# The 128 gram products of an image: three groups at every second quarter step in place of six groups at every quarter

## The chip, the cores and the metric

The kernel runs on one core of a Trainium2 chip. The metric is the device time of one execution in microseconds, the median of several executions. One profiled execution gives the page and the trace. Names: PE is TensorE (PEld its weight loads), DVE is VectorE, ACT is ScalarE, POOL is GpSimd, SP is the engine that issues most DMAs.

## The reference, cut to what matters

The input x has 16 images of 64 channels and 128 x 128 pixels, in float32. Four layers follow each other; each adds its result to x, after a group norm of 32 groups:

```python
# layer 0: gram matrix of the normalised image, applied to the image
gram = jnp.einsum('bcn,bdn->bcd', xf, xf) / N
y = jnp.einsum('bcd,bdn->bcn', gram, xf)
out = jnp.einsum('oc,bchw->bohw', conv_w, y)
...
x = x + _L0_conv_ref(_gn(x), L0_conv_conv_w)
x = x + _L1_conv_ref(_gn(x))          # |gx| + |gy| of a Scharr filter per channel
x = x + _L2_conv_ref(_gn(x), L2_conv_W, L2_conv_b)    # shift of half the channels, 3x3 convolution
x = x + _L3_conv_ref(_gn(x), ...)     # 3x3 and 1x1 convolution, batch norm over all images, clip
```

The change concerns the gram matrix alone: per image a 64 x 65 sum over 16384 pixels (the 65th column gives the channel sums).

## The kernel before, in words

An image is cut into NS = 8 chunks of R = 8 rows in each of its two halves. The main loop (lines 911 to 950) walks over steps, and in each step over four quarters, q = 0 to 3. In every quarter it calls, in this order, what each live stage has to do there: Layer3, Layer2, Front (layer 0's application and layer 1, with `sobel`), and last `Gram` (lines 926 to 930); then `tick()` (line 931) moves the small chains of statistics on by one link. Layer3 of image b starts at step 35 + 8b, Layer2 at 25 + 8b, Front at 15 + 8b (line 861), so that in the middle of the run one chunk of each of them is worked on in every step. All engines keep the order of the program (`InOrder`, line 63).

What PE gets in one step of the middle of the run, by quarter:
- q0, Layer3 (lines 814 to 821): `shared` into `one`, 6 matmuls, and `own` into `two[:, 0]`, 5 matmuls: 11.
- q1, Layer3 `own` into `two[:, 1]`, 5 matmuls (line 825), and Front `mix` into `po`, 2 matmuls (line 509): 7. In the last step before an image's grams two small ones for `pe` come along (line 508).
- q2, Layer2 `shared` and `own` (lines 742 to 747): 11.
- q3, Layer2 `own` (line 761), 5, and `mix` (line 524), 2: 7.

Every matmul has 128 rows of weights and 64 columns, and writes one half of the 128 output partitions. `issue` (lines 591 to 601) puts the two halves in turn, beginning with the half that was not used last (`last[0]`), so that two matmuls can run side by side. `own` (lines 611 to 620) has 3 matmuls on one half and 2 on the other.

DVE in the same step: at q0 `sobel`'s first two operations, the addition of edges to `two`, x3, and the difference d2 (line 702); at q1 four operations of `sobel`; at q2 Layer3's y (line 842), which reads `two` of q0 and q1, and d3; at q3 the second d3 and, after everything else, the difference d2 that the next q2 reads (line 769). This last one overwrites the buffer that q2's `own` matmuls read. ACT copies `po` into `xh` (lines 475 to 481), which frees the single `po` buffer for the next `mix`, and `one` into c (lines 767 and 828), which frees the single `one`.

`Gram` of an image (lines 407 to 444) loads eight slabs of x over SP, and ACT copies them into `xw`; at its step 8 and in the first half of its step 9 PE multiplies `xw` with itself, 128 matmuls of 64 columns of weights against 65 columns, accumulated in `pg`. They are put in groups at the end of quarters, after the work of the other stages. `n` counts quarters from step 8; at n = 6 `gram_chain` begins, with a DVE copy of `pg`. The next image's copies into `xw` begin at q3 of that step 9.

`pace` (lines 871 to 877) gives images 1 to 6 two sub-steps per quarter, so that two values of n fall into one quarter; images 0 and 7 to 15 have one. The gram step of images 7 to 15 is step 46, 54, ... 110 of the main loop, with all stages at work.

After the last y (step 163) come the batch norm's sums and a last stage of loads, one ACT and one DVE operation per part, and stores (lines 986 to 994).

Of the kernel before, what the change touches and what calls it, by code (L numbers as in the profile page):

```python
# [108 lines left out]
def tile_kernel(ctx: ExitStack, tc: tile.TileContext, x, cw_h, w2_t, b2, wbin_t, w1_t, b1, gamma, beta, consts, out):  # L109
# [297 lines left out]
    class Gram:  # L407
# [5 lines left out]
        def at(self, i, q):  # L413
            b = self.b
            CG = C // 8
            if i < NS:
                if q == 0 and i != 1:
                    for m in range(i + (1 if i == 2 else 2) if i else 0, min(i + 3, NS)):
                        t = xin.tile([P, CG, W], F32, tag="xr", name=f"xr_{b}_{m}", bufs=3)
                        sp.dma_start(t, x[b].rearrange("c h w -> h c w")[:, m * CG:(m + 1) * CG, :])  # L420
                        self.xr[m] = t

                if q == 3 and i > 0:
                    for m in (0, 1) if i == 1 else (i,):
                        act.copy(
                            xw[:, :, m * CG:(m + 1) * CG, :].rearrange("p w c t -> p c w t"),
                            self.xr.pop(m).rearrange("p c (w t) -> p c w t", t=2),
                        )
                return
            n = 4 * (i - NS) + q  # L430
            if n == 0:
                self.pg = ps_g.tile([P, CP, W], F32, tag="g", name=f"pg_{b}")[:, 0, 0:C + 1]

            for _ in range(22 if n < 4 else 20 if n < 6 else 0):
                w = self.w
                s = w % 2
                pe.matmul(
                    self.pg[s * C:(s + 1) * C, :], xw[:, w // 2, 0:C, s], xw[:, w // 2, :, s],
                    start=(w < 2), stop=(w >= W - 2),
                )  # L440
                last[0] = s
                self.w += 1
            if n == 6:
                chains.append(gram_chain(b, self.pg))
# [180 lines left out]
    class Layer2:  # L625
# [7 lines left out]
        def load(self, i):  # L633


            b = self.b
            N = (R + 1) * W + 2
            t = ring.tile([P, N], F32, tag="v2", name=f"v2_{b}_{i}", bufs=3)
            for c0, c1, shift in ((0, C // 4, 1), (C // 4, C // 2, -1), (C // 2, C, 0)):
                cut = R * W + 1 - shift  # L640
                parts = [(0, i * R, N)] if i + 1 < NS else [(0, i * R, cut), (cut, -R, N)]
                for at, j, end in parts:
                    for s in range(2):

                        first = j * W + at - 1 + shift
                        src = x2_d[b][W + first:W + first + 2 * C * PLANE].rearrange("(c s n) -> s c n", s=2, n=PLANE)
                        sp.dma_start(t[s * C + c0:s * C + c1, at:end], src[s, c0:c1, 0:end - at])
            self.v[i] = t[:, 1:N - 1].rearrange("p (j w) -> p j w", w=W)
            self.whole[i] = t
# [223 lines left out]
    for b in range(B):  # L873
        half = 1 <= b <= 2 * EARLY
        pace[b] = at, 2 if half else 1

        at += (NS // 2 if half else NS) + {0: 4, 2 * EARLY: 2}.get(b, 0)
# [33 lines left out]
    for step in range(steps):  # L911
        for q in range(4):
# [13 lines left out]
            for b in range(B):  # L926
                at, n = pace[b]
                for m in range(n):
                    v = 4 * n * (step - at) + n * q + m
                    run(Gram, b, v // 4, v % 4)  # L930
# [13 lines left out]
            if step >= last_one and q == 2:  # L944

                n = 3 if step == last_one else 1 if step < last_one + NS - 2 else 0
# [86 lines left out]
```

## Time and profile before

| | us |
|---|---|
| median of 3 runs | 2819.88 (2819.15 to 2820.23) |
| the profiled execution | 2818.68 |
| its span in the trace | 2816.9 |
| PE busy, weight loads busy | 2237.6, 1153.6 |
| DVE, ACT, POOL busy | 2201.0, 2121.1, 887.5 |
| first gram burst of images 7, 8, ... 15 begins at | 520.1, 658.7, 797.2, 935.7, 1074.2, 1213.0, 1352.1, 1490.6, 1629.1 |
| last stage, DMAs alone (2345 to 2817) | 472, at 402 GB/s |

Almost every instruction is recorded by one helper (line 73), so groups are told apart by their tiles: `pg<-xw` are the gram products, `two<-d,w`, `two<-qd,pk`, `two<-d,wi` the `own` matmuls, `one<-v,...` the `shared` ones, `po<-x,abd` is `mix`. Every matmul in float32 shows as two records. A record's length is not its share of PE's time, since matmuls are pipelined: the distance between starts is. In a line of the timeline the first number is the start, the second the length from the first start to the last end, then engine, line, operation and tiles, xcount; a bracket gives the idle time before it and what ended it, as inferred from semaphores. In a line of the waits stand the total, the number of times and the longest.

### The profile page before, as it was taken

The numbers are of one execution on the slowest core, as the hardware profiler recorded it, in microseconds if no ns is written. First come the engines' busy times: TensorE is split into PE (matmuls) and PEld (weight loads), VectorE is DVE, ScalarE is ACT, GpSimd is POOL, SyncE is SP. The second block draws the span as 40 slices with busy tenths as digits, with TensorE's granted clock in tenths as the row PEclk, the third lists the DMA queues.
The fourth block names the chain that finished last, engine by engine and source line by source line (L and its number), as shares of the span: only waits on it lengthen the run. The fifth ranks groups of instructions, "written<-read, shape, count | busy, mean of one in ns | idle before, by whom it ended". The sixth has DMA issues, their size and how long they took to land. (4 is left out here: it accounts for less than half of the span.)

```text
span 2816.9 us, 46299 instructions
## 1 busy us (share of the span) xinstructions
PE 2237.6 (79%) x14772; PEld 1153.6 (41%) x14772; DVE 2201.0 (78%) x3758; ACT 2121.1 (75%) x3171; POOL 887.5 (32%) x1326
## 2 busy tenths in 40 slices
PE   4568899999999999999999999999999995000000
PEld 2323444545554545353635363466666542000000
DVE  3999999898989898989898989999997435333332
ACT  4666779888888888888888888998997668333332
POOL 1035433343434343434343434454444310000000
PEclk7679999999999999999999999999999998555555
DMA  6789978888888888888888877787877767999999
GB/s 167 193 221 228 236 192 241 214 229 207 229 208 225 217 220 215 219 218 218 217 219 213 226 182 193 206 212 202 216 207 189 208 195 266 419 420 420 420 420 391
DMA packets 688880, 685.95 MB, mean 244 GB/s; under 512 B 61744, under 2 KB 590144, under 8 KB 688640
## 3 DMA queue, kind: packets, MB, share of 16 engines
q1 hardware_dynamic: 662656, 614.42, 73.6%
q0 software_dynamic: 24576, 68.12, 9.9%
q8 instruction: 119, 1.95, 0.3%
q14 instruction: 121, 0.99, 0.1%
q10 hardware_dynamic: 1408, 0.46, 0.1%
HBM read 346.23 MB, written 268.44 MB: 218 GB/s over the span
## 5 line engine op out<-in xcount | busy, mean ns | idle before, releaser
L73 PE MATMUL two<-d,w 128*64 128x508 f32 (+2 forms) x2560 | 889.8, 586 | 0.0
L73 PE MATMUL two<-d,wi 128*64 128x508 f32 (+3 forms) x1536 | 618.4, 577 | 0.0
L73 POOL DMA_DIRECT2D qd<-d x512 | 270.3, 530 | 867.1 <-issue 324.6
L73 PE MATMUL two<-qd,pk 128*64 128x512 f32 (+1 forms) x1024 | 518.9, 588 | 3.7 <-DMA qd<-d 3.0
L73 POOL TENSOR_SCALAR edges<-v,co 64x8 f32<-64x8 f32 x512 | 353.9, 691 | 357.5 <-ACT v L73 244.8
L73 PEld LDWEIGHTS two<-d,w 128*64 128x64 f32 x2560 | 303.3, 136 | 281.0 <-issue 200.3
L73 PE MATMUL po<-x,abd 128*64 128x512 f32 x1024 | 368.9, 631 | 60.6 <-ACT xh L73 60.6
L73 DVE TENSOR_TENSOR d<-v 128x512 f32<-128x512 f32 (+1 forms) x512 | 346.3, 679 | 75.5 <-issue 36.3
L73 PE MATMUL one<-v,w 128*64 128x508 f32 (+2 forms) x1600 | 391.8, 578 | 0.0
L73 PE MATMUL one<-v,wi 128*64 128x508 f32 (+3 forms) x1536 | 390.1, 593 | 0.0
L73 ACT COPY qd<-d 64x512 f32<-64x512 f32 x512 | 315.2, 616 | 21.0 <-DVE d L73 14.5
L73 DVE SCALAR_TENSOR_TENSOR e<-e 128x1032 f32<-128x1032 f32 (+1 forms) x256 | 313.0, 1223 | 0.0
L73 ACT ACTIVATE xh<-po,co 128x128 f32<-128x128 f32 (+1 forms) x480 | 275.3, 621 | 39.3 <-PE po L73 37.2
L73 PEld LDWEIGHTS two<-d,wi 128*64 128x64 f32 x1536 | 194.6, 135 | 146.2 <-issue 100.2
L73 DVE SCALAR_TENSOR_TENSOR y<-two,c 128x1024 f32<-128x1024 f32 x128 | 155.9, 1218 | 122.8 <-ACT v L73 65.8
L73 POOL TENSOR_SCALAR v<-v,kc 128x9 f32<-128x9 f32 x256 | 247.3, 980 | 12.0
L73 PEld LDWEIGHTS one<-v,w 128*64 128x64 f32 x1600 | 169.4, 137 | 160.4 <-issue 99.5
L73 ACT ACTIVATE v<-x,co 128x512 f32<-128x512 f32 (+2 forms) x368 | 234.8, 704 | 0.0
L73 PEld LDWEIGHTS one<-v,wi 128*64 128x64 f32 x1536 | 162.3, 138 | 154.9 <-issue 113.0
L73 ACT ACTIVATE u<-u 128x1024 f32<-128x1024 f32 x128 | 135.5, 1058 | 97.3 <-DVE u L73 96.8
L73 DVE SCALAR_TENSOR_TENSOR u<-xh 128x1170 f32<-128x1170 f32 x128 | 175.5, 1371 | 12.2 <-ACT xh L73 9.8
L73 PEld LDWEIGHTS pg<-xw 128*64 128x64 f32 x4096 | 161.6, 143 | 46.4 <-issue 38.6
(154 smaller groups left out, 3424.7 us busy)
## 6 DMA issues: line engine op xcount, KB each, us to landing
xr<-in_x SPq DMA_DIRECT2D x128, 512.0 KB, 6.9
x<-in_x SPq DMA_DIRECT2D x256, 256.0 KB, 4.2
x_d<-u SPq DMA_DIRECT2D x512, 128.0 KB, 3.6
y_d<-y SPq DMA_DIRECT2D x512, 128.0 KB, 4.2
x_d<-x SPq DMA_DIRECT2D x496, 128.0 KB, 2.5
qd<-d POOLq DMA_DIRECT2D x256, 130.0 KB, 3.0
qd<-d POOLq DMA_DIRECT2D x256, 129.8 KB, 3.7
v<-x_d SPq DMA_DIRECT2D x448, 72.1 KB, 3.0
```

The lines of the kernel that those rows point to most:

```text
L73: return self.tc.keep_in_program_order(call(*args, **kwargs))
```

## The change

The groups 22, 22, 22, 22, 20, 20 at n = 0 to 5 become 44, 42, 42 at n = 0, 2, 4. In a step and a half of images 7 to 15 the grams of q1 now stand at the end of q0, those of q3 at the end of q2, and those of the next q1 at the end of the next q0. Within each group the order of the products and of the halves is unchanged, and `gram_chain` still begins at n = 6.

```diff
             if n == 0:
                 self.pg = ps_g.tile([P, CP, W], F32, tag="g", name=f"pg_{b}")[:, 0, 0:C + 1]
 
-            for _ in range(22 if n < 4 else 20 if n < 6 else 0):
+            for _ in range({0: 44, 2: 42, 4: 42}.get(n, 0)):
                 w = self.w
                 s = w % 2
                 pe.matmul(
```

## Prediction

> **What bounds the kernel now.** I first read the page's 40 slices (TensorE, PE below, and VectorE, DVE, at 8 to 9 tenths from slice 4 to 32; after 2345 us the DMAs alone), then busy time by stretch, then the waits of one image's period. The gram bursts of images 7 to 15 begin every 138.5 us (520.1, 658.7, 797.2 ... 1629.1 us); I read the one at 797 us. q0 to q3 are a step's quarters; q0' and q1' are those of the next step. The gram step and a half runs from q0 at 792.90 to q2' at 825.94; the step before it has no grams.
>
> ```profile
> core 0: us, PE busy (x) PEld busy (x) DVE busy (x) ACT busy (x) POOL busy (x), PEclk, DMA share, GB/s
> 777.28:792.90 15.62, 15.62 (x79) 5.31 (x77) 15.25 (x22) 15.46 (x26) 7.41 (x10) 1.00 0.81 212
> 792.90:825.94 33.04, 33.04 (x368) 20.22 (x365) 26.20 (x35) 27.86 (x43) 10.58 (x20) 1.00 0.88 225
> ```
>
> The gram step leaves DVE and ACT idle; the step before it fills all three. The waits of DVE, then of PE, from 797 to 936:
>
> ```profile
> DVE y L73 <- ACT e L73: 4.0, 1, 4.0
> DVE d L73 <- issue: 3.5, 2, 1.8
> DVE d L73 <- POOL v L73: 0.8, 2, 0.5
> DVE two L73 <- PE two L73: 0.7, 1, 0.7
> ```
> ```profile
> PE po L73 <- ACT xh L73: 1.4, 1, 1.4
> ```
>
> So one image is a loop of two halves: PE sets the pace through the grams, DVE then works without pause, and PE meets it again in one wait of 1.35 us (at 914.89). Where PE hands over is in DVE's timeline:
>
> ```profile
> 824.19 1.23 DVE L73 SCALAR_TENSOR_TENSOR y<-two,c 128x1024 f32<-128x1024 f32 x1 [4.01 <-ACT e L73]
> ...
> 828.38 1.28 DVE L73 SCALAR_TENSOR_TENSOR u<-e,co,u 128x1024 f32<-128x1024 f32 x1
> 829.58 0.08 DVE L73 DVE_READ_ACCUMULATOR u<-e,co,u 128x1 f32 x1
> 831.36 0.56 DVE L73 TENSOR_TENSOR d<-v 128x384 f32<-128x384 f32 x1 [1.70 <-issue]
> ```
>
> The page names ACT e, done at 823.61; but y reads `two`, whose last q1' matmul starts at 823.50, lasts 0.59 and ends at 824.09, 0.10 before y. The d at 831.36 overwrites what q2' of PE reads, whose last matmul ends at 831.27. From there to 914.89 DVE is busy 81.0 of 83.5 us. So two dates set the period: **y** (end of q1') and **d** (end of q2'), with 1.70 us of slack between y's block and d.
>
> Now the joint between a quarter's work and its grams, PE's timeline at q0:
>
> ```profile
> 796.32 1.44 PE L73 MATMUL two<-d,w 128*64 128x508 f32 x5
> 797.17 0.34 PE L73 MATMUL pg<-xw 128*64 128x65 f32 x2
> 797.60 0.59 PE L73 MATMUL two<-d,w 128*64 128x508 f32 x1
> 798.02 1.55 PE L73 MATMUL pg<-xw 128*64 128x65 f32 x42
> 799.35 0.59 PE L73 MATMUL two<-d,w 128*64 128x512 f32 x1
> ```
>
> Each matmul is two records on one 64-column half of the array; two matmuls on different halves run side by side. Quarter q0 has 11 matmuls, an odd number: the last one (797.17 and 797.60) runs alone, with only one gram matmul (2 records) beside it, and the other grams begin when it is done.
>
> **What the Trainium skill says.** "TensorEngine Tiling (Array Packing)", Key Properties: tiles work independently and run matmuls in parallel. The trace agrees: pairs start within 0.01 us of each other. "TensorE: Matmul & The Clock Gate", Part 3, The mechanism, says that matmuls start and end strictly in program order; here the trace shows a little more freedom (2 to 4 gram records start before an earlier-issued matmul's last record), and the trace decides. The same page's table of specifications gives VectorE and ScalarE a strict first-in first-out queue: so everything on DVE behind y waits with it. The trace agrees (nothing in DVE's 4.01 us).
>
> **Prices.** A big matmul pair takes 0.853 us (795.46 to 796.32), so 0.427 per matmul. A gram matmul costs 0.063: 44 of them between two even pairs run from 282.17 to 284.94, 2.77 us, and the pair after them takes 0.86, as if no grams were there:
>
> ```profile
> 282.17 2.95 PE L73 MATMUL pg<-xw 128*64 128x65 f32 x88
> 284.94 1.03 PE L73 MATMUL po<-x,abd 128*64 128x512 f32 x4
> 285.80 2.94 PE L73 MATMUL pg<-xw 128*64 128x65 f32 x88
> ```
>
> So 22 grams are 1.39, 42 are 2.65, 20 are 1.26. What a quarter takes beyond that is the joint. The starts of q0, q1, q2, q3, q0', q1', q2' are 792.90, 799.35, 803.97, 810.43, 815.04, 821.37, 825.94. q0: 6.45 - 11 x 0.427 - 1.39 = 0.37. q1 (7 matmuls): 4.62 - 2.99 - 1.39 = 0.24. q2 0.38, q3 0.23, q0' 0.37 (20 grams), q1' 0.32, of which about 0.1 is a small statistics product. All six segments are odd; together about 1.9 us per image.
>
> **The change, part by part.**
> *Images 0 to 6.* Image 0's grams stand in one burst with no work between (256 records from 27.0 us). Images 1 to 6 run two sub-steps per quarter, so their groups are already 44, 44, 40 and become 44, 42, 42: 2 matmuls, 0.13 us, at most 0.8 us in six images; I take nothing.
> *The joints (nine images).* With grams after q0, q2 and q0' only, the segments are q1+q2 and q3+q0', 18 matmuls each, even. The joint at q0 stays (its segment begins long before, at the last product that spans both halves). The joints of q1, q2, q3 and q0', 0.24 + 0.38 + 0.23 + 0.37 = 1.22 us, go. Bounds of an even joint that isn't shown in this stage: nothing (the row at 284.94) to 0.2.
> *The grams that move ahead of q1'.* Before, 108 stand ahead of it; now all 128: +20 x 0.063 = 1.26 us. So **q1' starts at 821.37 - 1.22 + 1.26 = 821.41**. Its five Layer3 matmuls end at 824.13, y starts at 824.23: +0.04. In the first gram step the 22 grams moved ahead of q1 make y there 0.9 later and the grams moved ahead of q3 make `two` 0.6 later; both lie before the 4.01 us wait and are lost in it.
> *After y.* DVE's block from y to 829.66 ends at 829.70. PE reaches the end of q2' at 821.41 + 18 x 0.427 + 0.1 + 0.16 = 829.36 instead of 831.27, since q1' no longer has grams behind it. So **d starts at 829.74 instead of 831.36: -1.62 us**, and DVE's block, not PE, is now what ends last. ACT: its c (828.93, wait 0.96 on PE) and u (841.76, wait 0.62 on DVE) can move by 1.58 together, about the same.
> *Queues passed.* The grams issue no DMA. Their readers gain nothing: gs stays in its place (no wait at 827.65), ACT's xw copies at 831.83 wait for nothing. ACT work of q1 and q3 fed by the later matmuls (xh) has waits of 0.34 to 1.67 us ahead of it and lies before y or in its shadow.
> *Behind d.* DVE's 83.5 us up to PE's wait at 914.89 move as a whole. PE is ahead by 1.35 there; in its stretch after q1' it may lose one half slot (0.43) at the next product that spans both halves, which that lead hides. Without the lead it would cost 0.43 per image.
>
> Sum: -1.62 x 9 = **-14.6 us**. The profiled execution took 2818.7 (span 2816.9 and 1.8 around it): 2804.1. The median shown, 2819.9, is 1.2 higher: 2805.3; I say **2805**. The last stage (472 us, DMA share 1.00) is fixed in length and begins after the last y, so it moves along and hides nothing.
>
> **Rivals.**
> *More (B).* The half slot at q0 goes as well, if the halves arrive there in step: 0.37 more at y and d, -2.0 x 9 = -18: 2802; with a shorter DVE block down to 2799. Against: the profile shows the odd matmul at q0, and the work before it isn't changed.
> *Nothing (C).* The joints stay, as halves that are out of step lose the same half slots elsewhere. Then y is 1.26 later, its slack of 1.70 takes that, PE's d is unmoved: 2820. For: q1's five matmuls after grams run 0 1 0 1 1 by halves, out of step. Against: such a stream runs in the trace (po beside one at 858.57) at 0.427.
> *Slower (D).* A gram costs what a group's row suggests, 2.35 / 22 = 0.107, wherever it stands, and nothing is saved. Then y is 20 x 0.107 = 2.14 late, past the 1.58 that ACT and the 1.70 that DVE can take: +0.57 per image, 2825. It decides from y late by 1.6 on. Against: 44 in 2.77 us at 282.
>
> **Numbers.** Forecast (A) 0.64, own range 2801 to 2811 (even joints 0 to 0.2, three of them); B 0.12; C 0.14; D 0.10. A measurement here can tell about 0.2%, 5.6 us. A and B are faster: 0.76; C and half of D same: 0.18; rest slower: 0.06. Range 2799 to 2820: A, most of B, two thirds of C, 0.83.
>
> **What would show it.** Gram groups of 2.65 to 2.8 us without a lone two record beside them after q2 and q0'; q0 to q2' near 31.5 instead of 33.04; DVE's y wait still near 4 less 0.6, the wait of d gone or under 0.2; period near 136.9; PE's wait on xh still there. A y wait over 5 us makes D right; a period of 138.5, C. Wrong too if DVE finds a new wait in its long stretch.

## The result, and the profile after

| | before | after |
|---|---|---|
| median of 6 runs each, us | 2819.99 (2817.85 to 2820.28) | 2804.82 (2800.37 to 2805.94) |
| the profiled execution, us | 2818.68 | 2800.37 |
| its span in the trace, us | 2816.9 | 2798.6 |
| distance from one image's first gram burst to the next, us (images 7 to 15) | 138.51 to 139.05 | 136.76 to 137.33 |

The ratio is 0.9942, 95% interval 0.9931 to 0.9953: faster, by 0.58% in that ratio and by 15.2 us, or 0.54%, in the medians. The prediction was 2805. The profiled execution of the changed kernel is the fastest of its six; the extra 3.3 us lie before image 7, whose first burst begins at 516.8 instead of 520.1 us. Experiment e5 below shows that the change has no part in that, so the analysis goes by distances within one image. These give 13.8 us over the eight distances from image 7 to image 15 and 1.2 us after that.

The same image as before, by stretch: a step without grams, then from q0 to the start of q2', then DVE's long stretch from d to PE's restart:

```profile
core 0: us, PE busy (x) PEld busy (x) DVE busy (x) ACT busy (x) POOL busy (x), PEclk, DMA share, GB/s
770.46:786.08 15.62, 15.62 (x78) 5.21 (x76) 15.25 (x22) 15.46 (x26) 7.40 (x10) 1.00 0.79 209
786.08:817.33 31.25, 31.25 (x368) 17.62 (x365) 24.46 (x32) 26.92 (x41) 8.45 (x20) 1.00 0.86 217
822.86:906.37 83.51, 82.50 (x452) 36.81 (x448) 80.99 (x163) 75.89 (x119) 34.02 (x52) 1.00 0.85 224
```

The step without grams takes 15.62 us as before, and DVE's stretch 83.51 instead of 83.53. All of the gain is in the gram steps: from q0 to the start of q2' they take 31.25 us instead of 33.04.

The waits of DVE and then of PE in one image's period, from the first burst at 790.4 to the next at 927.2:

```profile
DVE y L73 <- ACT junk L73: 3.4, 1, 3.4
DVE two L73 <- PE two L73: 2.0, 1, 2.0
DVE y L73 <- ACT v L73: 0.9, 1, 0.9
DVE d L73 <- POOL v L73: 0.7, 2, 0.5
DVE d L73 <- issue: 0.3, 1, 0.3
```
```profile
PE po L73 <- ACT xh L73: 1.0, 1, 1.0
```

The wait of 4.0 in front of y is 3.4, `two` waits 2.0 instead of 0.7, and of d's two waits (1.8 and 1.7 before) 0.3 is left, the one of the first gram step. The wait for PE in front of the second d is gone, as DVE's timeline shows:

```profile
817.46 1.22 DVE L73 SCALAR_TENSOR_TENSOR y<-two,c 128x1024 f32<-128x1024 f32 x1 [3.44 <-ACT junk L73]
...
821.65 1.28 DVE L73 SCALAR_TENSOR_TENSOR u<-e,co,u 128x1024 f32<-128x1024 f32 x1
822.86 0.08 DVE L73 DVE_READ_ACCUMULATOR u<-e,co,u 128x1 f32 x1
822.86 0.56 DVE L73 TENSOR_TENSOR d<-v 128x384 f32<-128x384 f32 x1
```

No bracket stands on d: DVE goes from u straight to it. Now the joints on PE. Before the change the one of q2 looked like that of q0, a lone record with a single gram matmul beside it:

```profile
808.25 0.59 PE L73 MATMUL two<-d,wi 128*64 128x508 f32 x1
808.45 0.28 PE L73 MATMUL pg<-xw 128*64 128x65 f32 x2
808.68 0.59 PE L73 MATMUL two<-d,wi 128*64 128x508 f32 x1
809.11 1.49 PE L73 MATMUL pg<-xw 128*64 128x65 f32 x41
```

After the change, at q0 and at q2:

```profile
790.36 0.34 PE L73 MATMUL pg<-xw 128*64 128x65 f32 x2
790.78 0.59 PE L73 MATMUL two<-d,w 128*64 128x508 f32 x1
791.21 2.93 PE L73 MATMUL pg<-xw 128*64 128x65 f32 x86
793.94 0.59 PE L73 MATMUL two<-d,w 128*64 128x512 f32 x1
...
801.23 0.59 PE L73 MATMUL two<-d,w 128*64 128x508 f32 x1
801.26 0.59 PE L73 MATMUL two<-d,wi 128*64 128x508 f32 x1
801.65 2.79 PE L73 MATMUL pg<-xw 128*64 128x65 f32 x83
804.27 0.60 PE L73 MATMUL two<-d,wi 128*64 128x512 f32 x1
```

At q0 a lone `two` record still holds 86 of the 88 gram records back (790.78). At q2 the last two big records start side by side (801.23 and 801.26) and the grams follow 0.4 later, when both halves are free: 42 products take 2.62 us from 801.65 to the next big matmul.

### The profile page after: what moved, and what is told of

Its sections match the earlier page's. It is cut to its first block, busy times and chain, and to the rows that moved or that the text cites. A ratio compares the mean times of both kernels' runs of the same rounds, so it can differ in the third digit from the quotient of the medians.

```text
span 2798.6 us, 46299 instructions
## 1 busy us (share of the span) xinstructions
PE 2222.1 (79%) x14772; PEld 1088.8 (39%) x14772; DVE 2201.4 (79%) x3758; ACT 2120.1 (76%) x3171; POOL 859.5 (31%) x1326
## 5 line engine op out<-in xcount | busy, mean ns | idle before, releaser
L73 PE MATMUL two<-d,wi 128*64 128x508 f32 (+3 forms) x1536 | 626.6, 576 | 0.0
L73 POOL TENSOR_SCALAR edges<-v,co 64x8 f32<-64x8 f32 x512 | 335.2, 655 | 352.5 <-ACT v L73 244.4
L73 PE MATMUL po<-x,abd 128*64 128x512 f32 x1024 | 386.2, 631 | 60.4 <-ACT xh L73 60.4
L73 PE MATMUL one<-v,w 128*64 128x508 f32 (+2 forms) x1600 | 409.0, 578 | 0.0
L73 PE MATMUL one<-v,wi 128*64 128x508 f32 (+3 forms) x1536 | 407.4, 590 | 0.0
L73 POOL TENSOR_SCALAR v<-v,kc 128x9 f32<-128x9 f32 x256 | 238.4, 944 | 11.9
L73 PEld LDWEIGHTS one<-v,w 128*64 128x64 f32 x1600 | 163.3, 137 | 177.4 <-issue 130.0
L73 PEld LDWEIGHTS one<-v,wi 128*64 128x64 f32 x1536 | 156.0, 138 | 162.6 <-issue 126.4
L73 ACT ACTIVATE u<-u 128x1024 f32<-128x1024 f32 x128 | 135.4, 1058 | 90.3 <-DVE u L73 89.9
L73 PEld LDWEIGHTS po<-x,abd 128*64 128x64 f32 x1024 | 111.0, 140 | 175.4 <-ACT xh L73 92.3
```

What stands on the lines that cost most here:

```text
L73: return self.tc.keep_in_program_order(call(*args, **kwargs))
```

## The experiments

My theory has two parts. **Joints:** a group of grams costs most of a half slot wherever an odd number of big matmuls stands before it. (A lone big matmul takes as long as a pair, 0.85 us, and leaves the other half of the array empty; a half slot is the 0.43 us lost by that.) **Two dates:** the period follows y (the end of q1' on PE, then DVE's block) or d (the end of q2' on PE), whichever is later. The first rival is that fewer groups are better in themselves; the second, that y's later date is what holds the change back. In the first set (e1 to e4) the kernel before took 2820.09 us, in the second (e5 to e7) 2820.47, in the third (e8 and e9) 2819.54.

The period is the median of the eight distances from one image's first gram burst to the next; for e6 the range is given.

| | groups in images 7 to 15 | us | ratio to before, 95% | period, us |
|---|---|---|---|---|
| change | q0 44, q2 42, q0' 42 | 2804.8 | 0.9931 to 0.9953 | 136.8 |
| e1 | q1 44, q3 42, q1' 42 | 2804.1 | 0.9929 to 0.9957 | 136.7 |
| e2 | q0 44, q1 42, q2 42 | 2810.6 | 0.9955 to 0.9980 | 137.4 |
| e3 | six as before, idle half first | 2803.1 | 0.9928 to 0.9953 | 136.7 |
| e4 | q0 44, q2 42, q0' 22, q1' 20 | 2808.6 | 0.9949 to 0.9974 | 137.3 |
| e5 | six as before | 2820.2 | 0.9989 to 1.0005 | 138.6 |
| e6 | q0 128 | 2824.0 | 1.0008 to 1.0021 | 136.7 to 143.5 |
| e7 | q1 44, q3 42, q2' 42, chain later | 2790.1 | 0.9877 to 0.9908 | 135.4 |
| e8 | q0 64, q0' 64 | 2804.4 | 0.9931 to 0.9958 | 136.7 |
| e9 | as e1, chain later | 2794.9 | 0.9897 to 0.9924 | 136.0 |

### e1: the same three groups one quarter later

```diff
-            for _ in range({0: 44, 2: 42, 4: 42}.get(n, 0)):
+            for _ in range({1: 44, 3: 42, 5: 42}.get(n, 0)):
```

> Three groups, 44, 42, 42, at n = 1, 3, 5, at the ends of q1, q3 and q1'. Joint theory (a group costs a half slot of 0.24 to 0.38 us where an odd number of big matmuls stands between it and the last point at which both halves were in step): every segment now has 18 matmuls, q0's joint goes as well, all 1.8 us per image are saved on PE; y has only 86 grams ahead of it and comes about 3 us earlier against q0, so that d has a wait again, about 2.9 us, and PE's end of q2' sets it: period 138.53 - 1.81 = 136.7, time 2803 to 2804. Rival, that fewer groups save a fixed price each: as the change, 2805, with q0's joint no cheaper. Rival, that y's date is what limits the change: y is freed here, and the time falls below 2800.

Measured: 2804.06, period 136.65 to 137.20. Counted from q0, y comes at 27.89 us instead of 31.29 (about 3 us earlier was expected); DVE waits 2.04 in front of it, and 2.69 in front of d (expected about 2.9). All joints are even (no lone record stands beside the grams), and PE's date for d sets the period again. y is early and it doesn't help: the rival that y's date alone holds the change back, with a time below 2800, falls. The time can't tell the joints from a fixed price per group here (2804.06 and 2804.82); e2 and e3 do.

### e2: three groups again, at odd joints

```diff
-            for _ in range({0: 44, 2: 42, 4: 42}.get(n, 0)):
+            early = {0: 44, 2: 42, 4: 42}
+            late = {0: 44, 1: 42, 2: 42}
+            for _ in range((early if b < 7 else late).get(n, 0)):
```

> Images 7 to 15: also three groups, 44, 42, 42, but at n = 0, 1, 2, at the ends of q0, q1 and q2; images 0 to 6 as in the changed kernel. Joint theory: the joints of q0, q1 and q2 stay odd (0.37 + 0.24 + 0.38), only those of q3, q0' and q1' go; all 128 grams stand ahead of q1', so y is 1.26 - 0.60 = 0.66 later and d 0.8 to 0.95 earlier: 2811 to 2813. Rival, that the number of groups is what counts: 2805, as the change.

Measured: 2810.62, a little below the expected range: y comes 0.68 us later than before (expected 0.66) and d 1.11 us earlier (expected 0.8 to 0.95). With the same number and the same sizes of groups, about 6 us of the change's 15 are gone, as the joints say; the interval (0.9955 to 0.9980) and the change's (0.9931 to 0.9953) lie side by side without meeting, and the periods are 137.4 and 136.8. The number of groups is not what counts.

### e3: six groups at their old places, only the order of the halves changed

Against the kernel before the change:

```diff
-            for _ in range(22 if n < 4 else 20 if n < 6 else 0):
-                w = self.w
-                s = w % 2
+            count = 22 if n < 4 else 20 if n < 6 else 0
+            first = 6 if count and b > 6 else 0
+            halves = [1 - n % 2] * first + [0, 1] * ((count - first) // 2)
+            for s in halves:
+                w = self.done[s]
```

(xw is then indexed with w, start is w == 0 and stop the 64th product of a half; `done` counts per half.)

> The six groups of before at their old places, 22, 22, 22, 22, 20, 20; only within a group of images 7 to 15 the order differs: six products of the half that the odd big matmul leaves idle come first, then pairs. Joint theory: six instead of one or two gram products run in the shadow of the lone matmul, 4 to 5 x 0.063 = 0.25 to 0.31 us saved per joint, 1.7 us per image at d, and y is 1.4 us earlier: 2804 to 2807. Rival, that the number of groups is what counts: no change from before, 2820. Rival, that a half can't run ahead more than one or two products: 2818 to 2820.

Measured: 2803.06, about 1 us below the expected range and at least the whole gain of the change, with none of its moves; y comes 1.6 us earlier than before and d 1.8 (expected 1.4 and 1.7). PE's timeline at q0:

```profile
792.14 0.22 PE L73 MATMUL pg<-xw 128*64 128x65 f32 x1
792.14 0.59 PE L73 MATMUL two<-d,w 128*64 128x508 f32 x1
792.20 0.54 PE L73 MATMUL pg<-xw 128*64 128x65 f32 x6
792.57 0.59 PE L73 MATMUL two<-d,w 128*64 128x508 f32 x1
792.57 1.59 PE L73 MATMUL pg<-xw 128*64 128x65 f32 x37
793.94 0.59 PE L73 MATMUL two<-d,w 128*64 128x512 f32 x1
```

The lone matmul's two records (792.14 and 792.57) have gram records beside them all the time, on the half that stood idle before. The quarter takes 6.07 us from its start at 787.87 to 793.94; the bare sum of 11 x 0.427 + 1.39 was 6.08, and before the change it took 6.45. This is the strongest evidence for the joints: the hole itself was filled, and no group changed its place or its size.

### e4: the change with its last group split again

```diff
-            for _ in range({0: 44, 2: 42, 4: 42}.get(n, 0)):
+            for _ in range({0: 44, 2: 42, 4: 22, 5: 20}.get(n, 0)):
```

> The change with its last group split again: 44, 42, 22, 20 at n = 0, 2, 4, 5. Joint theory: the joints of q1, q2, q3 and q0' are saved as in the change, that of q1' isn't; y has 108 grams ahead of it and comes 1.2 us earlier than before; d is set by PE, 1.2 us earlier: 2809, with a wait of d of about 1.7 again. Rival, that the later y is what holds the change back: with y relieved, 2804 or less.

Measured: 2808.64. Both dates are as expected: y comes 1.22 us earlier than before, d 1.23, and d waits 1.69. Relieving y by 20 grams loses 4 us against the change, because the joint of q1' is odd again and PE reaches d later. (The two intervals overlap a little; the periods, 137.3 and 136.8, tell the kernels apart.) So relieving y gains nothing while PE's date for d is the later one.

### e5: only the images before the seventh

```diff
-            for _ in range({0: 44, 2: 42, 4: 42}.get(n, 0)):
+            early = {0: 44, 2: 42, 4: 42}
+            late = {0: 22, 1: 22, 2: 22, 3: 22, 4: 20, 5: 20}
+            for _ in range((early if b < 7 else late).get(n, 0)):
```

> Only images 0 to 6 get 44, 42, 42; images 7 to 15 keep 22, 22, 22, 22, 20, 20. My sum put nothing on these seven images: 2820, within 1 us, with first gram bursts of images 7 to 15 every 138.5 us. Rival, from the profile of the changed kernel, where image 7's first burst came at 516.8 instead of 520.1 us: 3.3 us of the gain arise before image 7, and this kernel takes about 2816.7.

Measured: 2820.23, no difference (0.9989 to 1.0005), image 7's first burst at 520.2. The 3.3 us at the head of the changed kernel's profile belong to that execution.

### e6: all 128 in one group

```diff
-            for _ in range({0: 44, 2: 42, 4: 42}.get(n, 0)):
+            for _ in range(({0: 128} if b > 6 else {0: 44, 2: 42, 4: 42}).get(n, 0)):
```

> Images 7 to 15: all 128 products in one group at the end of q0; images 0 to 6 as in the changed kernel. Joint theory with the two dates: PE loses only q0's joint, as in the change, and the same 128 grams stand ahead of q1'; but in the first gram step y, c and xh come 5 to 7 us later, which uses up the wait of y and makes ACT the last by about 0.3 us: period 138.5 - 1.35, time 2806 to 2810. Rival, that fewer groups are better in themselves: 2800 or less. Rival, that DVE starves for the 8 us of grams: slower than before, over 2820.

Measured: 2824.03, slower than before (1.0008 to 1.0021). My 2806 to 2810 was wrong, and the rival that gave over 2820 named the wrong cause: two of the eight periods are 136.72, as short as the change's, so the long waits of DVE for the first y that such a group brings (6.03 us in image 8) cost nothing. The others hold something else. PE's timeline of one image, and its stretches:

```profile
796.76 6.76 PE L73 MATMUL pg<-xw 128*64 128x65 f32 x208
807.35 2.75 PE L73 MATMUL pg<-xw 128*64 128x65 f32 x45 [3.83 <-issue]
```
```profile
core 0: us, PE busy (x) PEld busy (x) DVE busy (x) ACT busy (x) POOL busy (x), PEclk, DMA share, GB/s
796.80:803.50 6.70, 6.70 (x209) 6.57 (x207) 4.64 (x5) 6.70 (x12) 2.52 (x7) 1.00 1.03 258
803.50:807.30 3.80, 0.01 (x1) 0.00 (x0) 0.00 (x0) 1.02 (x2) 0.37 (x2) 0.84 1.10 265
807.30:811.00 3.70, 3.65 (x50) 3.24 (x52) 0.00 (x0) 0.00 (x0) 0.00 (x0) 0.50 0.24 64
811.00:815.00 4.00, 4.00 (x17) 2.14 (x15) 0.74 (x1) 0.00 (x0) 0.00 (x0) 0.76 0.37 111
```

After 210 of 256 records PE stops for 3.83 us with no semaphore to wait for, and comes back with a granted clock of 0.50. This image's period is 143.5 instead of 136.7 us: 3.8 are the stop, and by an estimate from the clocks in the rows above, 0.50 for 3.7 us and 0.76 for 4.0 us, the slower clock accounts for most of the rest. Six of the nine images have such a stop, of 1.65 to 3.83 us, after 161 to 230 records. Such a group uses up its instructions faster than at any other place: 256 matmul records and as many weight loads at 0.031 us each. In the trace a packet of 16 KB of the instruction queue q8 moves from 804.80 to 805.99, in the middle of this stop. The other five stops show the same: each time PE comes back 1.3 to 1.6 us after the end of such a packet. The queue moves 119 of them in the run, one for about 248 of the 29544 PE and PEld records, and the 256 matmul and 256 weight-load records of one such group pass in under 9 us where there is no stop. Of the three images without a stop, two (8 and 10) get a packet within the first 2.5 us of the group, and image 15 gets one after 6.6 us.

The kernel before holds one such group too, image 0's 256 records, and one short stop in it:

```profile
35.85 1.84 PE L73 MATMUL pg<-xw 128*64 128x65 f32 x52 [0.58 <-issue]
```

That group has a stop of 0.41 to 1.32 us in seven of the eleven profiled runs, each time after 204 records and 1.2 to 1.7 us after the end of a packet.

### e8: two groups of 64

```diff
-            for _ in range({0: 44, 2: 42, 4: 42}.get(n, 0)):
+            early = {0: 44, 2: 42, 4: 42}
+            late = {0: 64, 4: 64}
+            for _ in range((early if b < 7 else late).get(n, 0)):
```

> Images 7 to 15: two groups of 64 at n = 0 and 4, at the ends of q0 and q0'; images 0 to 6 as in the changed kernel. This asks why one group of 128 was slow. In that run PE stood still for 1.7 to 3.8 us in the middle of the group in six of nine images, after about 105 products, with no semaphore to wait for; the theory is that it had used up its instructions before the next ones were fetched. If so, a group of 64 has no such stall, the joints are those of the change, the same 128 products stand ahead of q1' and the time is the change's, 2804 to 2807. If what counts is that the products of a step stand so early that DVE and ACT starve, the time lies between, 2810 to 2815.

Measured: 2804.42, the change's time, with no stop inside any group of 64. So what made e6 slow is the length of the uninterrupted group: all 18 groups of 128 records pass, and six of nine groups of 256 stop. That PE waits for its instructions there is the likely reason: the dates of the packets fit every stop, but no run changed the fetching alone.

### e7 and e9: the last group behind q2'

e7's edit to the changed kernel is below; e9 has it too, with {1: 44, 3: 42, 5: 42} for `late`:

```diff
     def gram_chain(b, pg):
+        if b > 6:
+            yield
...
-            for _ in range({0: 44, 2: 42, 4: 42}.get(n, 0)):
+            late = {1: 44, 3: 42, 6: 42}
+            early = {0: 44, 2: 42, 4: 42}
+            for _ in range((early if b < 7 else late).get(n, 0)):
...
-            if n == 6:
+            if n == (6 if b < 7 else 7):
```

> Images 7 to 15: 44 and 42 products at n = 1 and 3 as in the run with odd quarters, but the last 42 at n = 6, behind the matmuls of q2' whose end frees d; gram_chain begins at n = 7 and its first link one quarter later still. Joint theory: d no longer has the last 42 grams ahead of it (2.65 us), one odd joint of 0.38 comes back at q2'; d's wait shrinks from 2.7 to under 0.6, DVE's long stretch begins earlier, and PE's own work sets the period: 135.3 + 0.4 = 135.7, PE's wait on xh near nothing, 2794 to 2797. Rival, that PE's total is what counts and d's date doesn't: 2804 plus 3, about 2807. Rival, that DVE's and ACT's readers of the grams (the copy of pg, the copies into xw) now wait: 2800 or more, with waits in front of gs or xw.

> The groups of the run with odd quarters (44, 42, 42 at n = 1, 3, 5), with gram_chain begun at n = 7 and one link later, as in the run whose last group stands past q2'. It asks which part of that run's further gain comes from the chain. If none, 2803 to 2805, with d's wait of about 2.7 us back; if the chain's DVE copy and products were in the way, under 2800.

e7 measured 2790.13, 14.7 us below the change and 4 us below its own forecast; of all versions it is the fastest. e9 measured 2794.85: I had no reason for a gain from the chain alone, and by the medians 9 of e7's 14 us beyond e1 came with it. DVE's waits in one period of e7, then of e9:

```profile
DVE y L73 <- ACT v L73: 3.1, 2, 2.2
DVE d L73 <- issue: 1.9, 2, 1.3
DVE two L73 <- PE two L73: 0.7, 1, 0.7
DVE d L73 <- POOL v L73: 0.2, 1, 0.2
```
```profile
DVE d L73 <- issue: 2.8, 1, 2.8
DVE y L73 <- issue: 2.0, 1, 2.0
DVE d L73 <- POOL v L73: 1.3, 2, 1.1
DVE me L73 <- PE bank L73: 0.4, 1, 0.4
```

In e9 d waits 2.8 and y 2.0, as in e1 (2.69 and 2.04): it is the other half of the loop that is shorter, 82.60 us from d (823.38) to PE's restart (905.98) instead of 83.53 in e1 (828.89 to 912.42). ACT and DVE just before that restart, in e1 and then in e9, show two links of the chain that matter:

```profile
906.87 1.22 DVE L73 TENSOR_TENSOR u<-u 128x1024 f32<-128x1024 f32 x1
908.12 1.06 ACT L73 ACTIVATE u<-u 128x1024 f32<-128x1024 f32 x1 [2.00 <-DVE u L73]
```
```profile
898.87 1.22 DVE L73 TENSOR_TENSOR u<-u 128x1024 f32<-128x1024 f32 x1
901.78 0.20 ACT L73 ACTIVATE sd<-var 128x1 f32<-128x1 f32 x1 [2.02 <-DVE var L73]
901.88 1.04 ACT L73 ACTIVATE u<-u 128x1024 f32<-128x1024 f32 x1
```

ACT's u is followed by its e, junk and `xh`, and `xh` is what PE waits for. In e1 the chain's last two links on DVE, three small operations up to `var` and nine from `r` to `co`, 1.9 us together, stand ahead of DVE's u; in e9 they stand behind it. A wait of 0.5 us in front of a d (`POOL v`) is gone too, and DVE's u starts 75.5 us after the stretch's first d instead of 78.0. ACT's u gains only 0.7 of that, since `sd`, which waits for `var`, now stands ahead of it on ACT. This is read from one period; no run moved these links alone.

The periods (136.0 and 136.7) account for 5.2 of the 9 us. In the two profiled executions another 4.2 lie before image 7's first burst (526.6 and 522.4), where both kernels have the same groups in images 1 to 6. Single executions differ there by more than that: image 6's first burst begins anywhere from 347.4 to 354.0 us in the eleven profiles, and e1's is the latest. So about 5 us can be put down to the chain. In e7 the wait of d in the second gram step is down to 0.59 and PE has no wait at all between 520 and 1660 us:

```profile
520.00:1660.00 1140.00, 1140.00 (x7907) 578.56 (x7905) 1065.84 (x1884) 1020.45 (x1597) 408.96 (x688) 1.00 0.84 221
```

The period, 135.4, is PE's own work, as the joint theory had it (135.7). From e9 to e7 only the last group moves, and the period falls from 136.0 to 135.4: the rival that d's date doesn't count falls, though about half of what e7's period gains over e1's belongs to the chain. ACT's copy into xw does wait, 1.9 us, and that is hidden.

## Why the prediction was right

*The sum.* -1.62 x 9 = -14.6 us was forecast, 15.2 measured. That the median lies within 0.2 us of 2805 is luck, as the six runs spread over 5.6 us. In the traces the period fell by 1.7 to 1.8 us; counted from the first burst, d comes 1.69 us earlier (34.19 to 32.50 us after it).

*Joints.* The working put q1' at 28.51 us after q0; in the changed kernel it is 814.64 - 786.08 = 28.56. The same prices put the start of q1 at 7.84, and it is 7.86; that of q3 at 18.18, and it is 18.19. So the price of a gram, 0.063, and even joints at nothing hold to 0.04 us per group. e2 leaves three joints odd, e4 two, and e3 fills the holes of all six; each came within 1 us of the time that the list of joints gives. One reading was too neat: pairs start within 0.01 us of each other in q0, but 0.06 apart in q1 (799.35 and 799.41).

*y's date.* y was to come 0.04 later against the start of q0 and comes 0.09 later (31.29 to 31.38 us after it). The 1.26 us of grams moved ahead of it are paid for by four joints, 1.22 us. The side steps were right too: y of the first gram step was to be 0.9 later and now waits 0.90 us, `two` 0.6 later, and the long y wait shrank from 4.01 to 3.44.

*d's date.* It was to have no wait, with DVE's block and not PE as the last; its bracket is gone, and e4 and e1, which free y, bring d's wait back (1.69 and 2.69). DVE's lead was over-estimated, though: the last q2' matmul on PE was to end 0.38 us before d and ends 0.20 before it (822.65 and 822.86), where 0.09 lay between the two before the change. So both dates now fall almost together.

*What hides what.* DVE's long stretch moved as a whole, 83.53 to 83.51 us. PE's wait at its end was 1.35 and is 1.01. The 0.34 that it lost is near the 0.43 of the half slot that was expected to reappear at the next product that spans both halves; no run isolated that loss.

*The rivals.* B had the joint at q0 gone; its lone record is still there. C and D had a period of 138.5 or more. The stop that made e6 slow was in none of them, although the trace before already had one of 0.58 us in image 0's group; groups of 44 lie well below the length at which it shows.

## What to carry to other kernels

When matmuls fill PE in pairs of halves, count them between the places where other work is put in: an odd count costs most of a half slot each time, 0.24 to 0.38 us here, and it can be won back by moving the insertion to an even place or by beginning the insertion with the idle half. Where two engines hand a period to each other, write down the dates at which one releases the other and the slack between them: work can be moved ahead of a date with slack at no cost, and what pays is taking work out of the stretch ahead of the date that comes last. Look for such dates behind waits that the profile names badly: here y's wait was put down to an ACT instruction and was PE's.

## What the runs showed of the hardware that was not expected

- A run of 256 gram records with their weight loads, 0.031 us apart, stops for 1.65 to 3.83 us in six of nine images of e6, after 161 to 230 records, and PE comes back 1.3 to 1.6 us after the end of a 16 KB packet of the instruction queue; the 18 runs of 128 records in e8 have no stop. After a stop of 3.83 us the granted clock is 0.50 for the next 3.7 us and big records take 1.06 us instead of 0.59.
- Products of one half don't hold to the program's order against the other half: before the change 2 to 4 gram records started ahead of an earlier-issued big record, and in e3 seven ran beside a lone matmul's first record (792.14 to 792.57).
- Moving a chain of small statistics by two ticks took 0.7 us off each period (136.7 in e1, 136.0 in e9); in the trace twelve small DVE operations, 1.9 us, went from ahead of an operation that ACT and PE wait for to behind it.
